# A four-layer network on one core: experts in groups of six and two samples, the first group sorted beside two attentions, norms and routing in finer steps

## The chip, the cores and the metric

The kernel runs on one core of one Trainium2 chip. The metric is the device time of one execution in microseconds (us), and the time before is the median of three runs. The engines are TensorE (PE, its weight loads PEld), VectorE (DVE), ScalarE (ACT), GpSimd (POOL) and SyncE (SP, which here only issues DMAs). Each engine works through its own queue in order.

## The reference

The input is eight samples of 256 channels by 32 x 32 positions, so 1024 tokens of 256 numbers for each sample, all in float32. Four layers follow each other: an attention and convolution block with a Fourier step (layer 0), a deformable convolution block (layer 1), a causal attention with a feed-forward over half of the tokens (layer 2), and a layer 3, which is the one that the change touches:

```python
t = t + _L3_attn_ref(_ln_t(t), ...)   # 8 heads; scores squared: square(s + 5) over its sum
t = t + _L3_ffn_ref(_ln_t(t), ...)    # 8 experts, each token goes to 2

def _moe(tokens, router_w, w1, b1, w2, b2):
    probs = softmax(tokens @ router_w.T)
    rw, re = top_k(probs, 2)
    rw = rw / maximum(rw.sum(-1), 1e-12)
    combine = zeros((N, E)).at[arange(N)[:, None], re].set(rw)
    out = tokens
    for e in range(E):
        h = gelu(tokens @ w1[e] + b1[e])
        out = out + combine[:, e:e + 1] * (h @ w2[e] + b2[e])
    return out
```

`_ln_t` is a layer norm of each token over its 256 channels.

## The kernel before

The layers are generators (`fast0` to `fast3e`), run one after the other. A tile has 128 partitions; a sample is 8 tiles of 128 tokens. An instruction that the kernel does not pin may be put ahead of its place by the program builder, on its own engine, when its inputs allow it; `pinned` instructions of one engine keep their order.

Two helpers order work that lies side by side. `spread(main, others)` takes the steps (yields) of a main generator and deals the steps of the others evenly between them. `by_time(streams)` gives each stream a due time and a period, and always takes the stream that is due first.

**Attention of layer 3** (`fast3`, from 3001 us on). For each sample `b`, `attention(b)` has 33 steps. In each of the first 32, PE makes the scores of four heads (`s`, L2605), ACT squares them into `e` (L2611, two instructions), and PE adds up the values of the step before (`A`, L2589); twice in a sample comes a projection (`proj`) that DVE adds to `x` (L2600). Beside it `spread` deals the steps of `between(b)`: routing of the sample before (`routes.route(b - 1)`), then the norm of the next sample (`norm`) and its `projections`. `spread` is told how many steps those are.

**Routing** (`Routes.route`): a norm (`token_norm`, L1002 to L1014: statistics on DVE, Ln and Exp on ACT, scaling on DVE), a store of the normed tokens to DRAM (`mox`), a sum on POOL (`x<-x,mo_x`, L2318) that is stored as `mos`, a transpose, the router's logits on PE (`mo_l`), the softmax (its Exp on ACT is L2337, `pr<-pr`), the two best experts, their weights, and each token's place among those of its expert (`mo_n`, `place`, `carry`).

**Groups and sort.** The samples are in two groups:

```python
GROUPS = ((0, 5), (5, 8))
```

When all of a group's samples are routed, `sort(g)` works out where each token goes in a buffer `so` that has the tokens of each expert together, in tiles of 128 rows. A group has 16 tiles for each sample and 7 to spare: 87 and 55. Then it takes one step for each tile of tokens (8 for each sample): SP loads the tile twice from `mox` into a row tile `xl` (L2423), POOL writes the destination beside it (L2427), and POOL issues two indirect DMAs (`so<-xl,rows`, L1021) that scatter the rows. The row tiles come from a pool of two buffers for the first sort and of six for the second. `sort(0)` is one of the streams beside attention 6, with 41 steps.

**Experts** (`fast3e`). The tiles of a group are taken in pairs, 44 in group 0 and 28 in group 1, each in two steps of `experts()`: SP loads `xs`, four pairs ahead; PE transposes (`a`, L2745), DVE copies (`xk`, L2747); ACT copies the expert's first weights (L2730); PE multiplies (`h`, L2759), ACT applies Gelu (L2765); PE multiplies again (`y`, L2781), DVE adds the bias (L2785), and POOL scatters the result to `res` with two indirect DMAs (L1021). The first load of a group waits for all scatters of its sort. Beside group 0 run the routing of the last sample and `sort(1)`, as one stream `rest`; beside group 1 runs `combine(0)`, which loads the results of group 0 (`yg`) in order of tokens, adds them by weight to the sums (L2847), transposes (`oT`, L2858) and stores the output. `combine(1)` follows when all experts are done.

```python
by_time([[0, 1, (next(all_pairs) for _ in range(n))], [1, n / 37, rest]])
by_time([[0, 1, all_pairs], [4, n1 / 36, combine(0)], [n1, 1, (next(last) for _ in range(1))]])
```

Of the kernel before, what the change touches and what calls it, by code (L numbers as in the profile page):

```python
# [12 lines left out]
AF = mybir.ActivationFunctionType  # L13
# [4 lines left out]
P = 128  # L18
B = 8
# [878 lines left out]
class Fast:  # L898
# [93 lines left out]
                dst[:, :, cols], x[:, :, cols], ps.unsqueeze(1).to_broadcast([P, KC, HF]), ALU.mult  # L992
            )

    def token_statistics(self, r, x, pool, pinned=lambda *_: None):

        nc = self.nc
        n = x.shape[1]
        st = pool.tile([P, n, 6], F32, tag="tn_s", name="tn_s")
        mv = pool.tile([P, n, 2], F32, tag="tn_m", name="tn_m")  # L1000
        for t in range(n):
            nc.vector.bn_stats(st[:, t, :], x[:, t, :])  # L1002
            nc.vector.bn_aggr(mv[:, t, :], st[:, t, :])
        pinned(nc.scalar.activation(r[:, 0], mv[:, :, 1], AF.Ln, bias=self.eps5))
        pinned(nc.scalar.activation(r[:, 0], r[:, 0], AF.Exp, scale=-0.5))
        nc.vector.scalar_tensor_tensor(r[:, 1], mv[:, :, 0], -1.0, r[:, 0], ALU.mult, ALU.mult)

    def token_norm(self, dst, x, pool):

        n = x.shape[1]  # L1010
        r = pool.tile([P, 2, n], F32, tag="tn_r", name="tn_r")
        self.token_statistics(r, x, pool)
        for t in range(n):
            self.nc.vector.tensor_scalar(  # L1014
                dst[:, t, :], x[:, t, :], r[:, 0, t : t + 1], r[:, 1, t : t + 1], ALU.mult, ALU.add
            )
# [45 lines left out]
def spread(main, others):  # L1062


    (gen, n), rest = main, [[g, m, 0] for g, m in others]
    for i in range(n):
        for r in rest:
            while r[2] < r[1] and r[2] * n <= i * r[1]:
                next(r[0], None)
                r[2] += 1  # L1070
        next(gen, None)
    for g in [gen] + [r[0] for r in rest]:
        for _ in g:
            pass


def by_time(streams, until=None):
# [926 lines left out]
def fast2f(net, io):  # L2004
    tc, nc = net.tc, net.nc
# [4 lines left out]
    with ExitStack() as ctx, ExitStack() as mid:  # L2010
# [26 lines left out]
        def before(b):  # L2037
            x = one.tile([P, KC, N], F32, tag="x", name="x")
            nc.sync.dma_start(out=x, in_=io.src[b])
            xt = one.tile([P, NT, C], F32, tag="xt", name="xt")  # L2040
            yield
            for t4 in range(0, NT, 4):
                ps = pair("xT")
                for i in range(4):
                    for c in range(KC):
                        nc.tensor.transpose(
                            ps[:, i * C + c * P : i * C + (c + 1) * P], x[:, c, bass.ts(t4 + i, P)], net.ident
                        )
                net.pinned(nc.scalar.copy(xt[:, t4 : t4 + 4].rearrange("p t c -> p (t c)"), ps))
                yield  # L2050
            r = norms.tile([P, 3, NT], F32, tag="r", name="r")
            net.token_statistics(r, xt, norms, net.pinned)
            nc.vector.tensor_scalar(r[:, 2], r[:, 0], 1.0, None, ALU.add)
            yield

            xn = xns[b] = three.tile([P, NT, C], F32, tag="xn", name="xn")
            s = ss[b] = four.tile([P, NT, C], F32, tag="s", name="s")

            def scaled(d, i):
                for t in range(NT):  # L2060
                    net.pinned(
                        nc.scalar.activation(
                            d[:, t, :], xt[:, t, :], AF.Identity, scale=r[:, i, t : t + 1], bias=r[:, 1, t : t + 1]
                        )
                    )
# [12 lines left out]
            yield  # L2078
            yield from scaled(s, 2)
            ps = pair("wrow")  # L2080
            for t in range(NT):
                nc.tensor.transpose(ps[:, bass.ts(t, P)], wcol[:, t : t + 1].to_broadcast([P, P]), net.ident)
            wrow = one.tile([P, N], F32, tag="wrow", name="wrow")
            net.pinned(nc.scalar.copy(wrow, ps))
            yield

            cnt = two.tile([P, 3, NT], F32, tag="cnt", name="cnt")
            nc.vector.memset(cnt[:, 1, 0:1], 0.0)
            for t in range(NT):
# [13 lines left out]
                yield  # L2103
            rank = cnt[:, 0]
            nc.vector.tensor_tensor(rank, rank, cnt[:, 1], ALU.add)
            nc.vector.tensor_tensor(rank, rank, cnt[:, 2], ALU.add)
            m = ms[b] = four.tile([P, NT], F32, tag="m", name="m")
            nc.vector.scalar_tensor_tensor(m, rank, PICKED - 0.5, wcol, ALU.is_lt, ALU.mult)
            idx = idxs[b] = four.tile([P, 2, NT], I32, tag="idx", name="idx")
            nc.vector.tensor_copy(idx[:, 0], rank)  # L2110
            nc.vector.tensor_scalar(idx[:, 1], rank, S - 1.0, None, ALU.min)
            yield
# [112 lines left out]

GROUPS = ((0, 5), (5, 8))
GROUP_OF = [g for g, (lo, hi) in enumerate(GROUPS) for _ in range(lo, hi)]
TILES = [2 * (hi - lo) * N // P + 7 for lo, hi in GROUPS]  # L2230
WIDEST = max(hi - lo for lo, hi in GROUPS)
# [5 lines left out]
class Routes:  # L2237
# [69 lines left out]
    def route(self, b, x, ones, pair):  # L2307
# [5 lines left out]
            return v.unsqueeze(2).to_broadcast([P, NT, E8])  # L2313

        xn = ones.tile([P, NT, C], F32, tag="xt", name="mo_x")
        net.token_norm(xn, x, two)
        nc.sync.dma_start(out=self.normed[b], in_=xn)
        nc.gpsimd.tensor_tensor(x, x, xn, ALU.add)  # L2318
        nc.sync.dma_start(out=self.sums[b], in_=x)
# [6 lines left out]
            nc.vector.tensor_copy(xk[:, c, :], ps)  # L2326
            yield

        ps = pair("mo_l")[:, 0]
        for t in range(NT):  # L2330
            net.linear(ps[:, bass.ts(t, E8)], xk, self.wr, bass.ts(t, P), slice(0, E8))
        pr = two.tile([P, NT, E8], F32, tag="pr", name="pr")
        nc.vector.tensor_copy(pr, ps[:, : NT * E8].rearrange("p (t e) -> p t e", e=E8))
        red = two.tile([P, NT], F32, tag="red", name="red")
        nc.vector.tensor_reduce(red, pr, AX.X, ALU.max)
        nc.vector.tensor_tensor(pr, pr, each(red), ALU.subtract)
        nc.scalar.activation(pr, pr, AF.Exp)  # L2337
        nc.vector.tensor_reduce(red, pr, AX.X, ALU.add)
        nc.vector.reciprocal(red, red)
        nc.vector.tensor_tensor(pr, pr, each(red), ALU.mult)  # L2340
# [101 lines left out]
def fast3(net, io):  # L2442
# [4 lines left out]
    with ExitStack() as ctx, ExitStack() as att, ExitStack() as bef:  # L2447
# [39 lines left out]
        def norm(b):  # L2487
# [1 line left out]
            nc.sync.dma_start(out=halves(x), in_=tokens(io.src[b]))  # L2489
            yield  # L2490
            xt = one.tile([P, NT, C], F32, tag="xt", name="xt")
            net.token_norm(xt, x, norms)
            nc.gpsimd.tensor_tensor(x, x, bo.unsqueeze(1).to_broadcast([P, NT, C]), ALU.add)
            yield
            xn = xns[b] = one.tile([P, KC, N], F32, tag="xn", name="xn")
# [78 lines left out]
        def attention(b):  # L2574
# [40 lines left out]
            values(len(steps) - 1)  # L2615
            yield

        def between(b):

            if b:  # L2620
# [20 lines left out]
        for b in range(B):  # L2641
            if b == B - 1:
                bef.close()
            beside = [(between(b), 17 * (b + 1 < B) + (8 if b else 6))]
            first = GROUPS[0][1]
            if b == first + 1:
                beside.append((routes.sort(0), 1 + NT * first))
            spread((attention(b), 33), beside)
        att.close()
        late = ExitStack()  # L2650

        def rest():
            routes.rows_of = io.pool(late, "mox2", 6)
            yield from routes.route(B - 1, xs[B - 1], one, lambda name: net.lent["pair"](name))
            yield from routes.sort(len(GROUPS) - 1)

        net.left = rest(), late
        late.push(ctx.pop_all())

def fast3e(net, io):
# [4 lines left out]
    with ExitStack() as ctx:  # L2668
# [196 lines left out]
                        sums(b + 3)  # L2865
                    yield

        rest, space = net.left
        all_pairs = experts()
        n = 2 * sum(g == 0 for g, _ in pairs)  # L2870
        n1 = 2 * len(pairs) - n
        by_time([[0, 1, (next(all_pairs) for _ in range(n))], [1, n / 37, rest]])
        space.close()
        sum_pool, y_pool = io.pool(ctx, "f3es", 3), io.pool(ctx, "f3ey", 5)
        last = combine(1)
        by_time([[0, 1, all_pairs], [4, n1 / 36, combine(0)], [n1, 1, (next(last) for _ in range(1))]])
        for _ in last:
            pass

# [270 lines left out]
```

## Time and profile before

| what | us |
| --- | --- |
| median of three runs (4435.02 to 4451.55) | 4436.91 |
| the profiled execution, its own time | 4446.59 |
| span of the profile, first to last instruction | 4444.7 |
| first square `e` of layer 3 | 3001.0 |
| last `x<-proj` of attention 5, 6, 7 | 3821.5, 3953.0, 4044.8 |
| first row of `sort(0)` on POOL | 3832.6 |
| first expert transpose `a` on PE | 4044.6 |
| last expert addition `y` on DVE | 4403.4 |

The durations in the prediction come from the profiled execution. A row of the timeline reads: start, length, engine, source line, operation, output from input, count, and in brackets the idle time before it with what ended it. Granted clock is the share of full speed at which PE was allowed to run.

### The profile page before, as it was taken

To read this page: it belongs to the slowest core of one execution; us is meant where nothing else is said; L and a number is where in the kernel's file an instruction comes from. 1 tells how busy PE (TensorE), PEld (TensorE's weight loads), DVE (VectorE), ACT (ScalarE), POOL (GpSimd) and SP (SyncE) were. 2 spreads that over 40 slices of the span, in tenths; PEclk is the share of its full clock that TensorE was granted. 3 is DMA by queue.
4 is the path that set the end of the run, shared out by engine and by line. 5 is a ranking of instruction groups with operands and counts; after the bars stand their busy time and mean duration, and the time that the engine had idled before them with its cause. 6 is when DMAs were issued, how large, how long until landed. Compare 5 with 4: busy or idle time off the path is not lost. (4 is left out here: it accounts for less than half of the span.)

```text
span 4444.7 us, 52329 instructions
## 1 busy us (share of the span) xinstructions
PE 4017.9 (90%) x19836; PEld 1911.5 (43%) x19836; DVE 2316.8 (52%) x3935; ACT 2146.1 (48%) x2736; POOL 555.6 (13%) x634
## 2 busy tenths in 40 slices
PE   8989999999887899989999978888999999999887
PEld 3223333333333444444444435553333443336776
DVE  2387777777888677742222266622333223324355
ACT  3454445444443466634334364425555555566443
POOL 0000000000000000000000023330000000353753
PEclk9999999999998999999999989999999999999997
DMA  2212222222222111010001023362100000236666
GB/s 85 77 50 83 87 73 88 81 76 80 69 89 82 58 59 49 31 41 19 20 19 38 10 88 105 97 207 76 34 29 29 10 20 29 75 122 201 183 221 244
DMA packets 188423, 348.44 MB, mean 78 GB/s; under 512 B 23706, under 2 KB 132460, under 8 KB 176644
## 3 DMA queue, kind: packets, MB, share of 16 engines
q1 hardware_dynamic: 165396, 293.31, 20.4%
q0 software_dynamic: 19104, 46.45, 3.0%
q10 hardware_dynamic: 3664, 5.24, 0.3%
q8 instruction: 160, 2.62, 0.2%
q14 instruction: 99, 0.81, 0.1%
HBM read 174.24 MB, written 152.04 MB: 73 GB/s over the span
## 5 line engine op out<-in xcount | busy, mean ns | idle before, releaser
L1230 DVE SCALAR_TENSOR_TENSOR a<-hp,w_f_vec,a 128x992 f32<-128x992 f32 (+1 forms) x512 | 627.9, 1232 | 150.2 <-ACT a L1223 142.6
L2611 ACT ACTIVATE e<-s,five 128x1024 f32<-128x1024 f32 x512 | 539.3, 1110 | 274.2 <-PE s L2605 273.7
L2605 PE MATMUL s<-q,k 32*128 32x512 f32 x2048 | 368.5, 673 | 20.0 <-ACT e L2611 17.9
L1363 ACT ACTIVATE e<-s 128x1024 f32<-128x1024 f32 x256 | 249.6, 1020 | 229.0 <-PE s L1357 228.9
L2589 PE MATMUL A<-e,v 128*32 128x512 f32 x2048 | 296.9, 635 | 17.8 <-ACT e L2611 17.8
L1319 DVE TENSOR_TENSOR sum<-sum,e 128x1024 f32<-128x1024 f32 x192 | 230.7, 1219 | 115.9 <-ACT e L1363 115.9
L1323 PE MATMUL A<-e,va 128*32 128x512 f32 x2048 | 288.7, 602 | 0.0
L78 PE MATMUL pi<-xn,w_l_wpi 128*128 128x512 f32 x512 | 248.0, 629 | 36.9 <-ACT e L1363 20.0
L1357 PE MATMUL s<-q,k 32*128 32x512 f32 x1024 | 195.1, 643 | 12.8 <-DVE xn L1219 7.1
L2605 PEld LDWEIGHTS s<-q,k 32*128 32x128 f32 x2048 | 116.7, 191 | 202.5 <-issue 82.8
L1398 ACT ACTIVATE hp<-pi,pib 128x1024 f32<-128x1024 f32 x64 | 71.4, 1115 | 234.6 <-PE pi L78 228.7
L78 PEld LDWEIGHTS pi<-xn,w_l_wpi 128*128 128x128 f32 x512 | 97.8, 200 | 177.9 <-issue 110.4
L1681 PE MATMUL pos<-pos,w_f_sel 64*128 64x512 f32 x576 | 163.7, 633 | 5.4 <-ACT ay L1707 2.1
L2759 PE MATMUL h<-xk,w 128*128 128x128 f32 x1136 | 145.5, 283 | 20.4 <-DVE xk L2747 20.2
L1021 POOL DMA_INDIRECT res<-y,to x142 | 143.5, 1011 | 123.0 <-issue 87.3
L2730 ACT COPY w<-w_l3f_w 128x512 f32 x142 | 88.3, 624 | 144.1 <-PE h L2759 142.3
L2759 PEld LDWEIGHTS h<-xk,w 128*128 128x128 f32 x1136 | 142.1, 198 | 26.9 <-DVE xk L2747 20.2
L78 PE MATMUL h<-xk,w_l2f_w 128*128 128x512 f32 x256 | 125.5, 648 | 27.9 <-DVE xk L2136 27.9
L1274 POOL MEMSET thrice<- 32x128 f32 x32 | 6.3, 196 | 1117.4 <-PE pe L1290 1072.3
L1323 PEld LDWEIGHTS A<-e,va 128*32 128x32 f32 x2048 | 61.3, 109 | 193.8 <-issue 191.5
L2589 PEld LDWEIGHTS A<-e,v 128*32 128x32 f32 x2048 | 42.5, 110 | 234.2 <-issue 201.7
L1021 POOL DMA_INDIRECT so<-xl,rows x128 | 129.5, 1012 | 90.5 <-DMA xl<-mox 62.7
(397 smaller groups left out, 7032.9 us busy)
## 6 DMA issues: line engine op xcount, KB each, us to landing
x<-d SPq DMA_DIRECT2D x32, 1024.0 KB
xs<-so SPq DMA_DIRECT2D x70, 260.0 KB
so<-zero SPq DMA_DIRECT2D x5, 3380.0 KB
thrice<-v SPq DMA_DIRECT2D x256, 64.0 KB
gated<-st SPq DMA_DIRECT2D x32, 512.0 KB
hc<-gated SPq DMA_DIRECT2D x32, 512.0 KB
d<-x SPq DMA_DIRECT2D x16, 1024.0 KB
xl<-mox SPq DMA_DIRECT2D x64, 256.0 KB
```

The lines of the kernel that those rows point to most:

```text
L78: self.nc.tensor.matmul(ps, lhsT=w[:, i, m], rhs=src[:, i, cols], start=(i == 0), stop=(i == k - 1))
L1021: made = self.nc.gpsimd.indirect_dma_start(**args)
L1230: nc.vector.scalar_tensor_tensor(to, fr, taps(t_), to, ALU.mult, ALU.add)
L1319: nc.vector.tensor_tensor(half, half, e[j], ALU.add)
L1323: nc.tensor.matmul(state["A"][32 * h : 32 * h + 32, c, :], lhsT=vas[b][:, kt, c, 32 * h : 32 * h + 32], rhs=e[h // 2][:, h % 2, :], start= ...
L1357: nc.tensor.matmul(ss[h // 2][:, h % 2], lhsT=ks[b][32 * h : 32 * h + 32, bass.ts(kt, P)], rhs=qs[b][32 * h : 32 * h + 32, bass.ts(gq, HF) ...
L1363: nc.scalar.activation(es[i][j], ss[j], AF.Exp, scale=SCALE)
L1681: nc.tensor.matmul(ps[:, bass.ts(h, HF)], lhsT=sel[r, t, xy, :], rhs=poss[b][r, :], start=True, stop=True)
L2589: nc.tensor.matmul(A[32 * h : 32 * h + 32], lhsT=v[:, kt, c * P + 32 * h : c * P + 32 * h + 32], rhs=e[:, h, :], start=first, stop=last,)
L2605: nc.tensor.matmul(ss[h // 2][:, h % 2], lhsT=k[32 * h : 32 * h + 32, c, bass.ts(kt, P)], rhs=q[32 * h : 32 * h + 32, c, bass.ts(hh, HF)], ...
L2611: nc.scalar.activation(e[:, 2 * j : 2 * j + 2], ss[j], AF.Square, scale=SCALE, bias=five)
L2759: nc.tensor.matmul(ps[:, j, m], lhsT=ws[j][:, k, bass.ts(m, P)], rhs=xk[:, j, k], start=(k == 0), stop=(k == KC - 1),)
```

## The change

`GROUPS` becomes six and two samples, so there are 103 and 39 tiles, 52 and 20 pairs, and the last two samples are combined at the end instead of three. `sort(0)` can now start only in attention 6, whose `between` routes sample 5: it begins 12 steps in (`later`), makes 16 of its 49 steps there and the other 33 or 34 beside attention 7. The norms become generators with a yield after the statistics and after Ln and Exp, which are pinned everywhere; in the routing the logits come in two halves with a yield between, and the softmax's Exp has a step of its own and is pinned. The step counts that `spread` is told follow: 19 for norm and projections, 12 for routing. Beside the experts of group 0, routing and `sort(1)` become two streams, the sort due from step 16 on at a period of 4.2.

```diff
-    def token_statistics(self, r, x, pool, pinned=lambda *_: None):
+    def token_statistics(self, r, x, pool):
...
             nc.vector.bn_aggr(mv[:, t, :], st[:, t, :])
-        pinned(nc.scalar.activation(r[:, 0], mv[:, :, 1], AF.Ln, bias=self.eps5))
-        pinned(nc.scalar.activation(r[:, 0], r[:, 0], AF.Exp, scale=-0.5))
+        yield
+        self.pinned(nc.scalar.activation(r[:, 0], mv[:, :, 1], AF.Ln, bias=self.eps5))
+        self.pinned(nc.scalar.activation(r[:, 0], r[:, 0], AF.Exp, scale=-0.5))
         nc.vector.scalar_tensor_tensor(r[:, 1], mv[:, :, 0], -1.0, r[:, 0], ALU.mult, ALU.mult)
+        yield
...
+def some(gen, n):
+    return (next(gen, None) for _ in range(n))
+
+def later(n, gen):
+    yield from range(n)
+    yield from gen
...
-GROUPS = ((0, 5), (5, 8))
+GROUPS = ((0, 6), (6, 8))
...
-        ps = pair("mo_l")[:, 0]
-        for t in range(NT):
-            net.linear(ps[:, bass.ts(t, E8)], xk, self.wr, bass.ts(t, P), slice(0, E8))
         pr = two.tile([P, NT, E8], F32, tag="pr", name="pr")
-        nc.vector.tensor_copy(pr, ps[:, : NT * E8].rearrange("p (t e) -> p t e", e=E8))
+        for t4 in range(0, NT, 4):
+            ps = pair("mo_l")[:, 0]
+            for i in range(4):
+                net.linear(ps[:, bass.ts(i, E8)], xk, self.wr, bass.ts(t4 + i, P), slice(0, E8))
+            nc.vector.tensor_copy(pr[:, t4 : t4 + 4], ps[:, : 4 * E8].rearrange("p (t e) -> p t e", e=E8))
+            if not t4:
+                yield
         red = two.tile([P, NT], F32, tag="red", name="red")
         nc.vector.tensor_reduce(red, pr, AX.X, ALU.max)
         nc.vector.tensor_tensor(pr, pr, each(red), ALU.subtract)
-        nc.scalar.activation(pr, pr, AF.Exp)
+        yield
+        net.pinned(nc.scalar.activation(pr, pr, AF.Exp))
+        yield
...
-            beside = [(between(b), 17 * (b + 1 < B) + (8 if b else 6))]
+            beside = [(between(b), 19 * (b + 1 < B) + (ROUTE if b else 6))]
             first = GROUPS[0][1]
-            if b == first + 1:
-                beside.append((routes.sort(0), 1 + NT * first))
+            if b == first:
+                sort = routes.sort(0)
+                n, early = 1 + NT * first, 16
+                beside.append((later(ROUTE, some(sort, early)), ROUTE + early))
+            elif b == first + 1:
+                beside.append((sort, n - early + 1))
...
-        by_time([[0, 1, (next(all_pairs) for _ in range(n))], [1, n / 37, rest]])
+        by_time([[0, 1, some(all_pairs, n)], [1, 1.1, routing], [16, 4.2, r.sort(1)]])
...
-        by_time([[0, 1, all_pairs], [4, n1 / 36, combine(0)], [n1, 1, (next(last) for _ in range(1))]])
+        by_time([[0, 1, all_pairs], [4, n1 / 43, combine(0)], [n1, 1, some(last, 1)]])
```

More of the change, by code (lines that the diff above doesn't have):

```diff
@@ L1003, in token_statistics, with token_norm_steps @@
             nc.vector.bn_aggr(mv[:, t, :], st[:, t, :])
-        pinned(nc.scalar.activation(r[:, 0], mv[:, :, 1], AF.Ln, bias=self.eps5))
-        pinned(nc.scalar.activation(r[:, 0], r[:, 0], AF.Exp, scale=-0.5))
+        yield
+        self.pinned(nc.scalar.activation(r[:, 0], mv[:, :, 1], AF.Ln, bias=self.eps5))
+        self.pinned(nc.scalar.activation(r[:, 0], r[:, 0], AF.Exp, scale=-0.5))
         nc.vector.scalar_tensor_tensor(r[:, 1], mv[:, :, 0], -1.0, r[:, 0], ALU.mult, ALU.mult)
-    def token_norm(self, dst, x, pool):
+        yield
+    def token_norm_steps(self, dst, x, pool):
         n = x.shape[1]
         r = pool.tile([P, 2, n], F32, tag="tn_r", name="tn_r")
-        self.token_statistics(r, x, pool)
+        yield from self.token_statistics(r, x, pool)
         for t in range(n):
@@ L2051, in before @@
             r = norms.tile([P, 3, NT], F32, tag="r", name="r")
-            net.token_statistics(r, xt, norms, net.pinned)
+            for _ in net.token_statistics(r, xt, norms):
+                pass
             nc.vector.tensor_scalar(r[:, 2], r[:, 0], 1.0, None, ALU.add)
@@ L2315, in route @@
         xn = ones.tile([P, NT, C], F32, tag="xt", name="mo_x")
-        net.token_norm(xn, x, two)
+        yield from net.token_norm_steps(xn, x, two)
         nc.sync.dma_start(out=self.normed[b], in_=xn)
@@ L2491, in norm @@
             xt = one.tile([P, NT, C], F32, tag="xt", name="xt")
-            net.token_norm(xt, x, norms)
+            yield from net.token_norm_steps(xt, x, norms)
             nc.gpsimd.tensor_tensor(x, x, bo.unsqueeze(1).to_broadcast([P, NT, C]), ALU.add)
@@ L2616, in attention @@
             yield
+        ROUTE = 12
         def between(b):
@@ L2650, in fast3 @@
         late = ExitStack()
[L2652 to L2657, printed above, removed]
+        net.left = routes.route(B - 1, xs[B - 1], one, lambda name: net.lent["pair"](name)), late
         late.push(ctx.pop_all())
+        routes.rows_of = io.pool(late, "mox2", 6)
 def fast3e(net, io):
@@ L2866, in combine @@
                     yield
-        rest, space = net.left
+        routing, space = net.left
         all_pairs = experts()
```

## The prediction, made before the run

> **What bounds the kernel now.** I read the page first (engine shares, the slices), then the last two layers stage by stage: busy time per attention, PE's idle gaps and who ended them, POOL's order of time around the sort, and the chain that ended last. The change reaches nothing before layer 3.
>
> ```profile
> span 4444.7 us, 52329 instructions
> PE 4017.9 (90%) x19836; PEld 1911.5 (43%) x19836; DVE 2316.8 (52%) x3935; ACT 2146.1 (48%) x2736; POOL 555.6 (13%) x634
> ```
>
> PE is the bound. Where it idles or runs slowly, time is to be had. Attentions 1, 4 and 6 and the whole of 7 (from one second-half `x<-proj` on DVE to the next):
>
> ```profile
> 3132.56:3270.86 138.30, 133.30 (x747) 53.72 (x745) 38.65 (x106) 78.89 (x79) 9.19 (x3) 0.95 0.08 28
> 3544.98:3683.58 138.60, 135.52 (x743) 54.65 (x743) 41.74 (x106) 76.87 (x77) 9.18 (x3) 0.94 0.06 24
> 3821.49:3952.97 131.48, 130.20 (x743) 53.57 (x743) 42.54 (x113) 76.59 (x75) 71.08 (x85) 0.97 0.39 123
> 3952.97:4044.76 91.79, 91.38 (x596) 33.13 (x597) 23.27 (x72) 69.98 (x71) 32.66 (x39) 0.96 0.50 162
> ```
>
> The columns are the stretch, its length, busy time of PE, PEld, DVE, ACT and POOL, granted clock, DMA share, GB/s. PE is 96 to 99% busy. What is lost is 3 to 5 us of gap per attention and a clock below 1. Attention 1 shows the cause, first on ACT, then on PE:
>
> ```profile
> 3156.17 0.26 ACT L2337 ACTIVATE pr<-pr 128x64 f32<-128x64 f32 x1 [9.38 <-DVE pr L2336]
> ```
> ```profile
> 3152.34 2.08 PE L2605 MATMUL s<-q,k 32*128 32x512 f32 x4
> 3157.48 2.07 PE L2605 MATMUL s<-q,k 32*128 32x512 f32 x4 [3.06 <-ACT e L2611]
> ```
> ```profile
> 3156.00:3160.00 4.00, 2.52 (x8) 0.70 (x12) 4.00 (x18) 3.27 (x4) 0.00 (x0) 0.50 0.00 0
> 3160.00:3164.00 4.00, 4.00 (x18) 0.71 (x12) 3.93 (x20) 1.55 (x4) 0.00 (x0) 0.50 0.00 0
> ```
>
> The router's Exp stands in ACT's queue before its logits exist, so ACT stops for 9.38 us, the squares `e` stop, PE starves for 3.06 us and then runs at clock 0.50 until about 3164. In the sort, POOL waits for each row tile (L2427 starts a row):
>
> ```profile
> 3954.31 0.23 POOL L2427 TENSOR_SCALAR xl<-w_f3e_dest 128x8 f32<-128x8 f32 x1
> 3957.74 1.04 POOL L1021 DMA_INDIRECT so<-xl,rows  x1 [3.20 <-DMA xl<-mox]
> 3959.09 0.97 POOL L1021 DMA_INDIRECT so<-xl,rows  x1 [0.30 <-issue]
> 3960.12 0.23 POOL L2427 TENSOR_SCALAR xl<-w_f3e_dest 128x8 f32<-128x8 f32 x1
> ```
>
> And the experts: start, beside the second sort, rest of group 0, group 1 in three stretches, tail.
>
> ```profile
> 4044.50:4102.00 57.50, 53.07 (x358) 49.73 (x355) 36.96 (x124) 29.68 (x72) 23.26 (x28) 0.91 0.63 206
> 4102.00:4248.00 146.00, 119.33 (x786) 105.78 (x784) 42.00 (x83) 63.52 (x168) 113.40 (x153) 0.99 0.57 173
> 4248.00:4280.00 32.00, 25.18 (x163) 23.43 (x164) 16.77 (x49) 12.52 (x33) 16.48 (x24) 0.87 0.49 153
> 4280.00:4335.00 55.00, 54.45 (x391) 51.09 (x390) 35.73 (x78) 33.54 (x82) 29.20 (x38) 1.00 0.91 303
> 4335.00:4343.00 8.00, 4.78 (x36) 4.23 (x34) 1.57 (x4) 3.21 (x7) 2.15 (x3) 0.93 1.03 398
> 4343.00:4403.50 60.50, 58.78 (x394) 54.31 (x394) 36.27 (x81) 31.33 (x76) 29.66 (x39) 0.95 0.69 228
> 4403.50:4444.70 41.20, 15.27 (x50) 8.86 (x50) 22.01 (x50) 6.08 (x6) 3.14 (x4) 0.54 0.63 234
> ```
>
> PE is full in group 1, but only 82% busy beside the second sort, where POOL (78% busy, the rest 0.28 to 0.30 us gaps between its instructions) sets the pace.
>
> **Part 1: finer steps in the attentions.** The built order puts the Exp after square 16 of an attention instead of 8, with the logits in two halves of 16 matmuls two steps ahead; the norm's Ln moves to square 30 of its own attention; and the load of sample 1 now stands ahead of the fill of the sorted buffers on SP. Attention 0 has an 11.99 us gap (ACT waited 12.55 us for that sample's statistics) and then a clock of 0.50 to 0.69 over 8 us, some 4 us: 16 in all. In attentions 1 to 5 PE's gaps before `s` are 3.06, 3.43, 3.63, 1.80 and 4.01, together 15.9. The clock costs there 6.9, 5.5, 5.5, 8.3 and 6.9 (one less the clock, times length), 33 less about 8 that lies inside the gaps; ACT's 2.2 us a step hides a little more, so 22. Together 54 us by the end of attention 5. Bounds: 15 if only attention 0 is mended, 62 if every dip goes. I take 54, since the order shows the cause of every gap removed. Attentions 6 and 7 give 3 to 4 us each, which lie behind Part 2. The added half-step work (8 more small copies, 0.2 us each) lies on DVE, 30% busy.
>
> The rows show the clock at 0.50 after a gap of 3.06 us, and in attention 7 from 3988 to 3992 with no gap at all, behind 32 tiny logits matmuls. The Trainium skill, "TensorE: Matmul & The Clock Gate", Part 1, puts the array at half rate after an idle window of about 3.4 us and back at full rate after about 3.4 busy us. By that page a stall would cost an estimated 1.7 us of clock, five of them 8.5 instead of 22, and the total below would be 13 us worse.
>
> **Part 2: the sort of group 0.** It has 48 row steps instead of 40, still with two row buffers, and can only start when sample 5 is routed, inside attention 6. On POOL the built order puts all rows behind the norm's `x` add of sample 7. From the start of attention 6: square 24 came 38 us in (3860), 35 without the stall; the counts, the sort's head, four samples' rows and the norm are some 18 us of DVE (the same for three samples ran 4087.0 to 4102.5); the add 4.5. So the first row is at 57.5. A row takes 4.38 us (33 of them from 3859.5 to 4004.1) or 4.15 (the last twelve); at 4.3, 47 take 202 and the last one's issue 3. On the way POOL does sample 6's add, 4.5. SP now issues the expert weights, 4.2 MB, and 2 MB of sample 6 in the middle of the rows; before, this came after them and held the DMA queues full from 4002 to 4025. I bound the delay by 0 and 18 us and take 10. Landing 3.2, and 3.9 from the load of `xs` to PE's first transpose (4040.7 to 4044.6). Sum 284: the experts start 284 us after the start of attention 6, where they now start 223 after it (4044.5 less 3821.5). So +61, of which Part 1 gives back 54: **+7**. PE idles for some 65 us between attention and experts; routing of sample 7 stands behind the first expert copies on DVE and does not fill it.
>
> **Part 3: the experts.** Warm, two tiles cost PE 3.95 us (1.78 + 0.44 + 1.73). POOL needs 2.77 for their two scatters (4105.82 to 4108.59) and 2.9 for a row, so one row to each pair made 5.67. The change gives two pairs to a row: 8.44 on POOL against 7.9. Group 0, now 52 pairs: 205.4, routing matmuls 7.3, start 4.7, clock at the start 5, POOL's excess 16 x 0.54 = 8.6, three more table loads at 1.28 of which 2 show, some 3 of the DVE stall of the check (9.09 and 2.38 us gaps at 4250 to 4261): 236. The same sum for before gives 244 where 235.5 was measured, so I take 232: **-3.5**, for eight more pairs. Bounds 222 and 248.
>
> Group 1 keeps 20 of 28 pairs: PE 79 and 12 output transposes of 0.87, 89.4. But six samples' combining now lies beside it. Bytes: 16 `xs` (four are loaded ahead) 4.3 MB, 41 scatters (two are group 0's last) 5.4, 24 `yg` 12.6, three sums (three are loaded ahead) 3.1, outputs 5.8, in all 31.2 MB; the row of 303 GB/s at share 0.91 makes 103 us, 398 makes 78. I take 105 with some stalls (95 to 120), against 123.5: **-18.5**. The Trainium skill, "DMA: Bandwidth & Descriptors", Specifications, gives about 358 GB/s of HBM per core, which speaks against packing the combine: it would make 87 us and leave PE the bound at 95 or so, 10 us better than the row I use; the 398 of one short stretch is above it.
>
> **Part 4: the tail.** Two samples instead of three after the last expert: 16 fewer adds of 0.46 is 7.4, and part of the waits for `yg` (4.64 and 6.10 us); I take **-9** of 41.
>
> Sum: 7 - 3.5 - 18.5 - 9 = -24. The profiled execution took 4446.6, 9.7 above the median of 4436.9; from the median the sum gives 4412.
>
> **Rivals.** (a) Slower: the row chain sets the experts' start and nothing is given back. If Part 1 returns only attention 0 and a little (20 us), the start moves by +41, and 41 - 31 is +10; with the weights' 18 us, +18, and with 4.38 a row +22, so 4459. It decides once Part 1 returns less than 30. For it: the chain is sure, its length is counted rows; against it: every gap has its cause named. (b) Group 1 becomes a DMA queue: DVE's adds wait for `yg` (as at 4335, a 6.87 us wait and a clock of 0.93) and hold the experts' copies, PE goes cold, 120 instead of 105: -9, 4428. For it: share already 0.91. (c) More is given back: 62 in the attentions, 4.15 a row (7), no weights bubble (8): -47, 4390. (d) That nothing moves is excluded by the built order.
>
> **Numbers.** The forecast (4398 to 4427) has 0.48, (c) 0.18, (b) 0.17, (a) 0.17. A measurement of this kernel tells 0.5%, 22 us, from no change: below 4415 lies two thirds of the forecast and (c), 0.50; slower is (a), 0.17; the rest, 0.33, is the same. The range runs from between (c) and the forecast's edge, 4385, to 4448, which leaves out half of (a) and some of (c).
>
> **What would show it.** Right: no `pr` wait of ACT over 1 us and no PE gap before `s` over 1 us in attentions 1 to 5, each at 126 to 130 us with clock 0.98 or more; POOL's rows 4.2 to 4.4 us apart, ending 50 us or more after the last `A`; a PE gap of 50 to 75 us before the first `a`; a pair per 4.0 to 4.3 us beside the second sort; DMA share near 1 in group 1. Wrong: attentions still at 135 (Part 1), a gap under 30 us (Part 2), group 0 over 248 or group 1 over 120 us (Part 3).

## The result and the profile after

The changed kernel took 4477.69 us (4473.65 to 4480.28, four runs) where the kernel before took 4438.69 in the same comparison: a ratio of 1.0078, interval 1.0063 to 1.0093. It is slower by 39 us. The forecast was 4412, the range ended at 4448.

The profiled execution took 4473.65 us, its span is 27.2 longer than that of before. (It lies 4 under its median, and the one of before lay 8 above its own, which makes up the rest of the 39.) Line numbers have moved by some twenty: L2625 is now the scores, L2609 the values, L2341 the transposed tokens' copy `mo_xk`, L2349 the logits' copy `pr`, L2356 the router's Exp, L1003 a norm's statistics, L2509 the load of a sample, L2769 and L2771 the experts' transposes and their copy.

```profile
span 4471.9 us, 52349 instructions
PE 3977.3 (89%) x19836; PEld 1915.0 (43%) x19836; DVE 2306.4 (52%) x3943; ACT 2149.4 (48%) x2739; POOL 558.1 (12%) x634
```

PE is busy 40.6 us less than before in a longer span: it waits more. By stages, attentions 2, 6 and 7 and what follows them (stretch, its length, busy PE, PEld, DVE, ACT, POOL, clock, DMA share, GB/s):

```profile
3257.70:3391.30 133.60, 127.26 (x744) 53.67 (x746) 39.86 (x108) 76.65 (x77) 9.20 (x3) 0.96 0.06 25
3793.98:3922.80 128.82, 126.07 (x743) 53.04 (x746) 44.87 (x139) 76.65 (x77) 49.05 (x56) 0.99 0.27 86
3922.80:4011.10 88.30, 87.86 (x594) 31.98 (x594) 24.79 (x83) 69.98 (x71) 41.35 (x51) 1.00 0.53 169
4011.10:4077.30 66.20, 0.00 (x0) 0.02 (x1) 2.98 (x9) 0.00 (x0) 31.70 (x42) 0.52 0.45 138
```

Attention 7 runs at clock 1.00; attention 2 still loses 6.3 us of PE and runs at 0.96. Then PE does nothing for 66 us, in which POOL works through the rows. The timelines of attention 2 show the new loss, on SP, on DVE, on PE and on ACT:

```profile
3270.93 0.32 SPq L2334 DMA_DIRECT2D mos<-x  x1
3274.74 0.32 SPq L2509 DMA_DIRECT2D x<-d  x1
```
```profile
3270.68 1.23 DVE L2341 COPY mo_xk<-mo_xT 128x1024 f32<-128x1024 f32 x1 [1.86 <-PE mo_xT L2340]
3279.54 0.75 DVE L1003 BATCH_NORM_STATS2 tn_s<-x 128x6 f32<-128x256 f32 x2 [7.64 <-DMA x<-d]
```
```profile
3272.89 1.95 PE L78 MATMUL mo_l<-w_l3f_wr,mo_xk 128*128 128x8 f32 x16
3282.99 3.37 PE L78 MATMUL mo_l<-w_l3f_wr,mo_xk 128*128 128x8 f32 x15 [6.09 <-DVE pr L2349]
```
```profile
3290.70 0.26 ACT L2356 ACTIVATE pr<-pr 128x64 f32<-128x64 f32 x1
```

Read from the bottom: ACT no longer waits for the Exp, the 9.38 us of before are gone. But PE had the first half of the logits done at 3274.8 and stands 6.09 us before the second half, for DVE's copy of the first. DVE was idle for most of that time: in its queue eight pairs of statistics stand ahead of that copy, and the first waits 7.64 us for a load. This is not the next sample's norm but that of the sample after it. Its load goes into the buffer that this very routing gives back with its store `mos`, 3.8 us before. Then the clock (windows of attention 2, same columns as above):

```profile
3278.00:3283.00 5.00, 0.01 (x1) 0.01 (x1) 3.40 (x17) 0.40 (x1) 0.00 (x0) 0.65 0.18 75
3283.00:3288.00 5.00, 5.00 (x24) 3.99 (x24) 0.64 (x3) 0.00 (x0) 0.00 (x0) 0.50 0.00 0
```

In attentions 1 to 5 these gaps are 9.18, 6.09, 6.08, 6.17 and 6.20 us, 33.7 together, where the gaps that went were 15.9. Behind attention 7, PE's first transposes name what they waited for:

```profile
4077.31 1.94 PE L2769 MATMUL a<-ident,xs 128*128 128x128 f32 x8 [66.24 <-DMA xs<-so]
```

The experts in six stretches, the last being the tail:

```profile
4077.30:4130.20 52.90, 44.79 (x273) 40.49 (x273) 29.65 (x102) 26.32 (x57) 18.20 (x20) 0.85 0.62 208
4130.20:4175.00 44.80, 44.80 (x301) 42.50 (x302) 16.08 (x32) 23.78 (x62) 30.07 (x41) 0.93 0.48 145
4175.00:4281.70 106.70, 98.74 (x682) 91.33 (x680) 39.11 (x85) 56.26 (x149) 81.67 (x112) 0.99 0.57 177
4281.70:4327.50 45.80, 43.56 (x291) 40.87 (x292) 20.69 (x47) 23.52 (x63) 23.72 (x34) 0.95 0.43 133
4327.50:4440.00 112.50, 90.41 (x597) 81.76 (x595) 66.94 (x152) 50.31 (x114) 42.61 (x55) 0.92 0.81 285
4440.00:4471.90 31.90, 9.52 (x32) 5.67 (x32) 14.43 (x33) 4.05 (x4) 2.44 (x4) 0.55 0.57 208
```

PE is full in group 0 only from 4130 to 4175 (85% busy before, 93 and 95% behind that), and group 1 has a DMA share of 0.81 with PE busy in 90 of 112.5 us.

### The profile page after: what moved, and what is told of

The parts are those of the page before. It is cut to its first block, busy times and chain, and to the rows that moved or that the text cites. A ratio compares the mean times of both kernels' runs of the same rounds, so it can differ in the third digit from the quotient of the medians.

```text
span 4471.9 us, 52349 instructions
## 1 busy us (share of the span) xinstructions
PE 3977.3 (89%) x19836; PEld 1915.0 (43%) x19836; DVE 2306.4 (52%) x3943; ACT 2149.4 (48%) x2739; POOL 558.1 (12%) x634
## 5 line engine op out<-in xcount | busy, mean ns | idle before, releaser
L2625 PE MATMUL s<-q,k 32*128 32x512 f32 x2048 | 348.5, 652 | 3.3 <-DVE x L2620 1.8
L2609 PE MATMUL A<-e,v 128*32 128x512 f32 x2048 | 280.1, 613 | 0.0
L1371 PE MATMUL s<-q,k 32*128 32x512 f32 x1024 | 194.3, 643 | 12.8 <-DVE xn L1233 7.1
L2625 PEld LDWEIGHTS s<-q,k 32*128 32x128 f32 x2048 | 111.2, 186 | 166.6 <-issue 93.7
L1024 POOL DMA_INDIRECT so<-xl,rows x128 | 129.4, 1011 | 113.2 <-DMA xl<-mox 78.6
L2805 PE MATMUL y<-w_l3f_w,hid 128*128 x568 | 140.5, 389 | 0.5 <-ACT hid L2789 0.5
```

The lines of the kernel that those rows point to most:

```text
L1024: made = self.nc.gpsimd.indirect_dma_start(**args)
L1371: nc.tensor.matmul(ss[h // 2][:, h % 2], lhsT=ks[b][32 * h : 32 * h + 32, bass.ts(kt, P)], rhs=qs[b][32 * h : 32 * h + 32, bass.ts(gq, HF) ...
L2609: nc.tensor.matmul(A[32 * h : 32 * h + 32], lhsT=v[:, kt, c * P + 32 * h : c * P + 32 * h + 32], rhs=e[:, h, :], start=first, stop=last,)
L2625: nc.tensor.matmul(ss[h // 2][:, h % 2], lhsT=k[32 * h : 32 * h + 32, c, bass.ts(kt, P)], rhs=q[32 * h : 32 * h + 32, c, bass.ts(hh, HF)], ...
L2805: nc.tensor.matmul(ps[:, j, :], lhsT=hid[:, j, k, :], rhs=w[:, k, :], start=(k == 0), stop=(k == KC - 1))
```

## The experiments

Fourteen more runs followed, twelve variants and the two kernels once more. In their comparisons the kernel before took 4478 to 4488 us, about 1% more than in the first one, so the ratios to it are compared, not the times. Stages are counted from one second-half `x<-proj` to the next, and of the experts from the first transposes of a group; they come from the one profiled execution of each run.

**One half of the change at a time.** First the groups and the early sort without the finer steps (`some` and `later` as in the change, with 8 for `ROUTE`), then the finer steps without the groups (old `GROUPS`, old sort, old `by_time` lines, with `n / 41` for the period of `rest`, whose routing has four more steps).

```diff
-GROUPS = ((0, 5), (5, 8))        # groups_only: this, and the diff's sort and by_time
+GROUPS = ((0, 6), (6, 8))
```

> The kernel before with the groups of six and two and the early first sort alone; norm, logits and routing in their old, coarse steps. Theory (the old losses in the attentions stay, about 3821 at the end of attention 5; the sort's chain is unchanged, so the experts start 284 us after the start of attention 6, at about 4105; group 0, group 1 and tail as in the changed kernel, +14.7, -11 and -9.3 against before): 61 - 6 = +55 against before, about 4494 us. Rival (the finer steps are what makes the changed kernel slow, the grouping itself costs nothing): within 10 of before, 4430 to 4450 us.

> The changed kernel with the finer steps alone; groups of five and three, the first sort beside attentions 6 and 7, and the by-time orders of before. Theory (the finer steps give about 27 us by the end of attention 5 and 34 by the end of attention 7, and nothing of that is given back, since the chain of 40 rows starts that much earlier too): 30 below before, 4405 to 4412 us; PE's gap ahead of the second half of the logits, 6 to 9 us, stands in attentions 1 to 5 here as well. Rival (the finer steps also cost the experts their slow start): 10 to 20 below before, 4420 to 4430 us.

Measured: groups_only 1.0134 (1.0116 to 1.0153), +59 us; steps_only 0.9945 (0.9928 to 0.9961), -29 us. Both are near their theories (+55 and -30). The product is 1.0078, the changed kernel's own ratio in the first comparison: the two halves add up, and the finer steps by themselves are a gain. In steps_only PE's gap ahead of the second half is there too (33.6 us over five attentions).

**The kernels before and changed, once more.** To have the stages of both in the later comparisons.

> The changed kernel once more, beside the three that follow, to have its stages on their chip. 0.7 to 0.9% above the kernel before, as in its first comparison. Group 0 took 241 us in its first profile, and 260 to 271 in three kernels with the same groups that ran elsewhere since. If that is the chip, it takes 255 to 265 here; if those kernels' own edits did it, 241 again.

> The kernel before once more, for its stages on the chip of the later runs. The changed kernel's group 0 took 241.5 us from its first transposes on the first chip (229.0 before) and 263.4 on the later one. If the longer time is the grouping's, before stays at 229 to 232 here; if it is the chip's, it takes 242 to 252, and the difference stays 12 to 20.

Measured: 1.0085 (1.0069 to 1.0101) and 0.9999 (0.9986 to 1.0011). From first transposes to first transposes group 0 took 252.7 us before and 263.4 changed; in the first comparison it was 229.0 and 241.5. So both are 22 to 24 longer in the later comparisons, whatever the kernel, and the grouping costs 10.7 and 12.5: the first alternative of the one expectation and the second of the other, though the difference lies below the 12 to 20 expected. The later comparisons ran on four different chips; the chip of the first is not known. DVE's waits in this part of before_again (total, times, longest) have an entry that the first profile of before lacks (after_again has it too, 17.8 us in 3 waits, and the first profile of the changed kernel does not):

```profile
DVE xk L2747 <- remote: 30.6, 5, 7.1
```

**The order on DVE.** The statistics of this layer's norms and the logits' copies keep program order, so that the copies come first.

```diff
-            nc.vector.bn_stats(st[:, t, :], x[:, t, :])
+            held(nc.vector.bn_stats(st[:, t, :], x[:, t, :]))     # held = self.pinned for layer 3's norms
...
-            nc.vector.tensor_copy(pr[:, t4 : t4 + 4], ...)
+            net.pinned(nc.vector.tensor_copy(pr[:, t4 : t4 + 4], ...))
```

> The changed kernel with one more order: on DVE the statistics of a norm of this layer and the copies of the logits stay in program order, so that no statistics stand ahead of the copies. Theory (PE's gap of 6 to 9 us ahead of the second half of the logits comes from the statistics of the sample after next, which DVE has ahead of the first half's copy and which wait for that sample's load): the gaps, 33.7 us over attentions 1 to 5, go, the attentions take 126 to 129 us instead of 133 to 137, and the whole is 30 to 40 below the changed kernel, 4438 to 4448 us, about the kernel before. Rival (the wait only moves: the statistics now wait for the load later and hold DVE's other copies, the projections' or the values', so that PE stands there): 4468 to 4480 us.

Measured: 0.9984 (0.9973 to 0.9994), which is 45 us below the changed kernel's 1.0085 in after_again and a little more than the theory's 30 to 40. Attentions 1 to 5 took 125.0, 125.0, 126.6, 126.6 and 125.0. First an attention of the changed kernel in the later comparisons (attention 3 of after_again), then attention 2 of the pinned one:

```profile
3412.50:3547.40 134.90, 128.50 (x743) 53.84 (x746) 39.81 (x108) 76.76 (x77) 9.20 (x3) 0.95 0.06 24
```
```profile
3259.70:3384.70 125.00, 124.75 (x743) 51.89 (x743) 41.04 (x107) 76.76 (x77) 9.20 (x3) 1.00 0.07 26
```

The same matmuls, the gap gone, the clock whole. The wait did not move elsewhere in attentions 1 to 5; attention 6 took 3.5 us more. So the statistics in front of the copy are shown to be what cost the changed kernel these 45 us.

**The same order in the kernel before.** Statistics, the single copy and the subtraction of the maximum pinned, nothing else.

> The kernel before with one order alone: on DVE the norms' statistics of this layer, the copy of the logits and the subtraction of the maximum stay in program order. Theory (ACT's 9.4 us at the router's Exp in attentions 1 to 5 came from the statistics of the sample after next, which stood ahead of the subtraction on DVE and waited for that sample's load; the place of the Exp on ACT is second to that): attentions 1 to 5 take 126 to 130 us instead of 137 to 139, and since the first sort and the experts move along, the whole is 40 to 50 below the kernel before. Rival (the Exp's place on ACT is the cause, as the prediction had it; it stands in front of squares whose scores are there): ACT's wait stays above 5 us, the attentions stay above 134, and the whole is within 15 of before.

Measured: 1.0070 (1.0054 to 1.0086), 31 us slower, so both expectations are wrong. ACT's wait at the Exp only fell from 32.5 to 21.8 us over five attentions; and the statistics of the router's norm, no longer taken early half by half, now stand on PE's path:

```profile
PE mo_xT L2325 <- DVE mo_x L1014: 10.7, 5, 2.5
```

The attentions took 139.7 to 147.0. A gap of 2.49 us ahead of `mo_xT` at 3440.76 was followed by this:

```profile
3440.00:3446.00 6.00, 5.24 (x11) 2.21 (x11) 2.84 (x9) 0.97 (x1) 3.05 (x1) 0.57 0.42 171
3446.00:3452.00 6.00, 6.00 (x19) 1.84 (x19) 1.22 (x1) 2.23 (x2) 1.46 (x1) 0.50 0.45 183
```

So the order on DVE is worth something only together with the finer steps. Why is not shown; our reading is that the norm's steps, which put Ln and the scaling later, give DVE the time.

**The Exp alone.** In the kernel before, the router's Exp one step behind the subtraction and one ahead of the sum.

```diff
+        yield
-        nc.scalar.activation(pr, pr, AF.Exp)
+        net.pinned(nc.scalar.activation(pr, pr, AF.Exp))
+        yield
```

> The kernel before with the router's Exp alone moved, a step behind the subtraction and a step ahead of the sum; norms and logits as before. In the built order the Exp stands two squares later on ACT, and the logits' copy and the subtraction stay ahead of most statistics on DVE. Theory A, the prediction's (the Exp's place on ACT is the cause of ACT's wait): ACT's 9.4 us fall under 3, attentions 1 to 5 take 128 to 133 us instead of 137 to 139, ratio 0.992 to 0.995. Theory B (the load that the statistics wait for is the cause, and the norm's Ln or the Exp still stands behind it on ACT): ACT waits 5 us or more for the Exp or the Ln, the attentions stay above 135, ratio 0.997 to 1.002.

Measured: 0.9962 (0.9948 to 0.9975), 17 us faster; attentions 2 to 4 took 132.3, 133.9 and 132.3, attentions 1 and 5 139.2 and 136.5. ACT's wait for the Exp fell from 32.5 to 4.2 us, its wait for the norm's Ln from 18.7 only to 13.9:

```profile
ACT tn_r L1004 <- DVE tn_m L1003: 13.9, 5, 4.1
ACT pr L2338 <- DVE pr L2336: 4.2, 1, 4.2
```

This lies between the theories, with the Exp's wait nearer to A and the ratio nearer to B: the Exp's place was a true cause, and what is left of ACT's wait is at the Ln. (The profiled execution lay 19 us above the run's median, so its stages are a rough guide.) In before_again DVE's statistics waited for a load 6.0 us over the five attentions, 5.7 of it in attention 1, so the load was a side matter there. It became the main one when the copies came to stand behind it.

**Undoing one finer step.** The norms in one step again (no `yield` in `token_statistics`, counts 17 and 10); the logits in one piece (one `mo_l`, one copy, count 11).

> The changed kernel with one of its finer steps undone: the norms again in one step (statistics, Ln and Exp, application); the logits stay in halves and the Exp of the router late. In the built order the first half's copy now stands ahead of the statistics on DVE, the second half's behind seven of their eight pairs. Theory (the new gap of PE comes from the norm's finer steps, which let the statistics of the sample after next slip ahead of the first copy): PE's gap ahead of the second half falls from 6 to 9 us to under 2, attentions 1 to 5 take 127 to 132 us instead of 134 to 136; attention 0 loses its repair again, 10 to 12 us; 10 to 25 below the changed kernel, ratio to before 1.003 to 1.006. Rival (the halves themselves make PE wait): the gap and 134 us an attention stay, and with attention 0 the ratio is 1.010 to 1.012.

> The changed kernel with the other finer step undone: the logits in one piece of 32 matmuls with one copy. The copy still stands behind the statistics on DVE in the built order. Theory (the statistics ahead of the copy are the cause, not the halves): the copy still waits 7 to 10 us, holds one of three PSUM buffers, and PE stands there at the scores instead of the second half; attentions 1 to 5 stay at 133 to 137, ratio to before 1.006 to 1.012. Rival (the halves are the cause): attentions 1 to 5 at 126 to 130 and the ratio under 1.002.

Measured: coarse_norm 1.0079 (1.0064 to 1.0094) with attentions of 130.1 to 135.4; logits_whole 1.0036 (1.0022 to 1.0050) with 129.8 to 135.0. In both PE's wait went from the second half of the logits to the scores and halved. PE's waits over attentions 1 to 5 (total, times, longest), in that order:

```profile
PE s L2624 <- DVE pr L2348: 17.5, 5, 5.8
```
```profile
PE s L2622 <- DVE pr L2348: 14.6, 5, 5.5
```

Against 33.1 in after_again. So neither step alone makes the gap; the two meet. By the ratio logits_whole fell between its theory and its rival, and coarse_norm below its rival and above its theory. Without the halves the changed kernel is 22 us faster: 16 in attentions 1 to 5, and the experts start 273.8 instead of 282.5 us after attention 5, since the sort starts earlier. What coarse_norm gained there, 11 us, was lost again behind them: the experts start 293.4 us after attention 5 instead of 282.5.

The two also differ in the clock. Over attentions 1 to 5 PE stood still for about as long in both, 19.6 us in coarse_norm and 15.9 in logits_whole, but the granted clock was 0.99 with the logits in halves and 0.96 with the 32 matmuls in one piece. The norm's steps differ too, so this suggests, and does not show, that the one piece costs clock by itself.

**Three row buffers for the first sort.**

```diff
-self.rows_of = io.pool(ctx, "mox", 2)
+self.rows_of = io.pool(ctx, "mox", 3)
```

> The changed kernel with three row buffers for the sorts in the attentions instead of two. Theory (a row's period of about 4.3 us is the load of its buffer behind the scatter that frees it; with a third buffer POOL's own 2.9 us a row set the pace): 47 rows are 60 us shorter, PE's gap of 66 us ahead of the experts falls under 10, and the whole is 50 to 60 below the changed kernel, 4418 to 4428 us. Rival (the period is POOL's and the queue's issue, not the buffers): the gap stays at 55 to 66, the whole within 10 of the changed kernel, 4468 to 4480 us. In between, with a period of 3.6: 33 us less, about 4445.

Measured: 1.0000 (0.9987 to 1.0014), 38 us below the changed kernel, with this ahead of the experts:

```profile
4051.32 1.94 PE L2769 MATMUL a<-ident,xs 128*128 128x128 f32 x8 [19.62 <-DMA xs<-so]
```

The 48 rows took 182 us from the start of the first to the last scatter, instead of 225 in the changed kernel's first profile. POOL's waits for the row loads fell from 78.6 to 22.0; but now POOL's add for sample 6, in the middle of the rows, waits 16.8 us for its norm on DVE, which the slower rows had hidden. That is why the rows gave 43 us, not 60, and the whole came out between the theory (50 to 60) and the middle case (33).

**Both repairs**, with either grouping.

> The changed kernel with both: the order on DVE and three row buffers. Alone they brought 45 and 35 us. Theory (two separate losses: the first in attentions 1 to 5, the second behind them): 80 below the changed kernel, 40 to 50 below the kernel before; the gap ahead of the experts 15 to 20 us. Rival (the sort's chain then waits for something else, the norm's add on POOL or the load of the expert weights): 50 to 60 below the changed kernel.

> The finer steps with the groups of five and three as before, the order on DVE and three row buffers. Theory (28.7 of the finer steps and 45 of the order add up, since here the sort of 40 rows ends beside attention 7 and hides): 65 to 75 below the kernel before; no gap over 3 us ahead of the experts; the third buffer brings nothing by itself. Rival (with shorter attentions the sort's chain is what ends last here too): 45 to 55 below.

Measured: 0.9905 (0.9889 to 0.9920) and 0.9852 (0.9834 to 0.9869), 42 us and 62 us below before. The repairs add up. And with both, groups of six and two are still 20 to 24 us slower than five and three: the experts start 247.9 us after attention 5 instead of 219.5, and group 0 takes 21.5 us more, against 11.1 less in group 1 and 6.9 in the tail; in these two profiles the remaining 12 us, in favour of six and two, lie before the end of attention 5.

**The combining's loads on another queue.**

```diff
-                    nc.sync.dma_start(
+                    nc.scalar.dma_start(
                         out=ys[n],
```

> The changed kernel with the combining's loads of expert results issued from ACT's queue instead of SP's. Theory (in group 1 DVE's 22.9 us of waiting for these loads come from SP, where they stand behind the loads of sorted rows, which wait 64.8 us for POOL): group 1 is 8 to 15 us shorter than the 122 us it takes from its first transposes to the last expert on such a chip, ratio to before 1.005 to 1.007. Rival 1 (the loads are bound by what DMA moves, 279 GB/s on the mean there): within 3 us, 1.008 to 1.009. Rival 2 (ACT stands in their waits and holds the experts): 5 us or more slower, above 1.0095.

> Finer steps, groups of five and three, the order on DVE and three row buffers, which ran at 0.9852 of before, and with them the combining's loads on ACT's queue. Theory of the SP queue: 3 to 8 us more, ratio 0.9835 to 0.9845, less than with groups of six and two since less is combined beside group 1. Rival: the same or slower, 0.985 or above.

Measured: yg_act 1.0087 (1.0071 to 1.0103), no change within the interval. In its profile DVE's waits for `yg` fell from 21.9 to 11.7 us and group 1 from 122.3 to 114.5, but group 0, where nothing was changed, took 10 us more; in the eight kernels with groups of six and two in the later comparisons it took 259 to 274 us, so 8 us can't be read from one profile. Inconclusive, then: the queue holds these loads up, but what it is worth is within the noise. best_yg came to 0.9832 (0.9819 to 0.9845), 76 us faster than before and the fastest of all; its interval overlaps that of the kernel without this edit.

## Why the prediction was wrong, step by step

| step | predicted | measured, in spans |
| --- | --- | --- |
| Part 1, by the end of attention 5 | -54 | -27.5 |
| Part 2, experts after the start of attention 6 | 284 | 283.3 |
| experts' start | +7 | +32.8 |
| group 0 | -3.5 | +12.4 |
| group 1 | -18.5 | -9.7 |
| tail | -9 | -8.4 |
| sum | -24 | +27.2 |

The last three stages end here at the same instructions in both kernels: group 0 where the prediction ended it, just behind POOL's last index conversion (`to<-xs`) of the group (4279.38 before, 4324.61 after), and group 1 with the last expert addition (4403.43 and 4438.98). The stretches of the profile above end 2.3 and 0.9 us later, and the expectations' +14.7, -11 and -9.3 come from those. Of the 51 us between -24 and +27.2, Part 1 makes 26.5, group 0 16 and group 1 9.

**Part 1 failed, in the step from "the order shows the cause of every gap removed" to 54 us.** Attention 0 was mended, 11.8 of the 16 us. In attentions 1 to 5 the gaps named were removed, too. What the step did not ask is what had come to stand ahead of the logits' copies: the statistics stand there (the rows of attention 2 above), and the prediction put the halves' cost at some 0.2 us copies on DVE, "30% busy". A mean share says nothing of an engine that works in order and has a load at its head. Of the 38 us for attentions 1 to 5, 15.8 came. The pin shows that the mechanism was under-priced if anything: without the new gap the five attentions take 628 us against 688 in before_again, 60 less.

The reading of the old gaps was too narrow as well. The prediction showed attention 1 and named the Exp's place on ACT. Of the 9.38 us there, DVE stood 5.58 at a statistic that waited for a load, ahead of the subtraction that the Exp needs. And in attentions 2 to 5 PE's gap came not behind the Exp but behind ACT's wait for the norm's Ln (4.03 to 4.66 us). From the profile before, attention 1 on DVE, then attention 3 on ACT and PE:

```profile
3155.59 0.43 DVE L1002 BATCH_NORM_STATS2 tn_s<-x 128x6 f32<-128x256 f32 x1 [5.58 <-DMA x<-d]
```
```profile
3435.12 0.30 ACT L1004 ACTIVATE tn_r<-tn_m,eps 128x8 f32<-128x8 f32 x1 [4.30 <-DVE tn_m L1003]
3436.71 1.57 PE L2605 MATMUL s<-q,k 32*128 32x512 f32 x4 [3.63 <-ACT e L2611]
```

The change moved the Ln too, so the gaps went; but the instruction that then cost 33.7 us, a statistic waiting for a load ahead of what others need, could be seen in the profile before.

**The clock term.** In its part on the clock the prediction set the rows (22 us for five dips) against "TensorE: Matmul & The Clock Gate", Part 1, of the Trainium skill (an estimated 8.5). The rows were nearer: over the five attentions the granted clock was 0.95 in before_again and 0.99 in the pinned kernel, some 28 us by the prediction's measure. Behind a gap of 2.49 us, below the page's idle window of about 3.4 us, PE ran at 0.57 and 0.50 for 12 us in which it was busy for 11.2, and behind 6.09 us it was at 0.50 for the first 5 busy us and at 0.78 on the mean of the next 4. In neither place was it back after 3.4.

A gap is not the only thing behind half clock, though. The prediction has PE starve for 3.06 us in attention 1 and then run at 0.50. In that attention the clock was at 0.50 before the gap, which begins at 3154.42, with PE busy all the time, behind the 32 logits matmuls that end at 3149.49:

```profile
3150.60:3154.40 3.80, 3.80 (x12) 0.58 (x10) 0.00 (x0) 0.00 (x0) 1.37 (x1) 0.50 0.94 282
```

So a part of the 22 us goes with the logits in one piece, which the change also cut in two, and not with the gaps; attention 7 has the dip and no gap, as the prediction says. That the one piece is the cause, and how much it costs, no run separates.

**Part 2 was right to a microsecond**, which is in part luck, with compensating parts: the first row came at 52.5 us (57.5 predicted), the rows started 4.65 apart on the mean, the add and all waits included (4.6 by the prediction's terms), and from the start of the last row to PE's first transpose it took 12.5 us (10.1). Rival (a) named what then happened: the chain sets the start, and it decides once Part 1 returns less than 30. It got 0.17; it should have had more, since the chain was a sure cost and the return a chain of guesses about four queues. The time ended above even its worst case, 4459, because group 0 and group 1 missed as well.

**Part 3, group 0.** The sum gave 236 and was lowered to 232 because the same sum overshot before. Measured, to the same end, 247.9. The pace beside the sort was priced right: POOL's rows came 8.41 to 8.48 us apart where two pairs went to a row (8.44), and without one stop of 5.46 us the 24 pairs from 4175 took 4.22 each. Two terms were too small. DVE's waits for the check's loads stopped PE for 5.46 and 2.23 us, where 3 were put: 4.7. And the clock was 0.85 over the first 52.9 us and 0.93 over the next 44.8, 11 us where 5 were put: 6. In this stretch PE also stopped for the head of the second sort, which DVE did ahead of the experts' copy, and then ran 16 matmuls in 3.78 us that take 1.95 at full clock:

```profile
4130.16 3.78 PE L2783 MATMUL h<-xk,w 128*128 128x128 f32 x16 [4.96 <-DVE xk L2771]
```

It is the same kind of stop as in Part 1, and the 4.7 put for the start covers its 4.96 us only by chance. Lowering a sum by the error of another, in a stage whose pace the change alters, was a further wrong 4 us.

**Part 3, group 1.** 113.8 instead of 105, inside the bounds and between the forecast and rival (b)'s 120: DVE's waits for `yg` stop PE for 4.35, 7.07 and 5.06 us. The DMA share was 0.81, where near 1 was the sign named.

**Part 4 was right**, 8.4 against 9.

## What to carry to other kernels

When a step is moved or cut finer and a builder decides the order, read the built order of every engine for what now stands ahead of the instructions that free a buffer, above all an instruction that waits for a load; a low busy share is no answer. A serial chain that is sure to get longer weighs more than a gain that needs several queues to behave. Where a gap is to go, look for the second instruction behind the first: here the Exp alone gave 17 us, the finer steps, which also move the Ln, 29, and the order alone cost 31, but steps and order together, with a third row buffer, gave 62.

## What the runs showed of the hardware that was not expected

- The same kernel took 1% longer in the later comparisons, with the granted clock at 0.948 against 0.952. Of its 39 us, 18.4 lie before the end of attention 0, and about 24 in group 0, where DVE's copies stood 30.6 us on a releaser that the trace only calls "remote". What that is was not found, nor whether the chip makes the difference.
- PE ran at half clock or little above for 12 us, of which it was busy for 11.2, behind a gap of 2.49 us (the kernel before with the order on DVE).
- PE ran at half clock behind 32 router matmuls of 128x8 with no gap at all: 3.80 us at 0.50 with PE busy for 3.80, before the gap of attention 1 of the kernel before began.
